# One neighbour fewer for the gather queue in every fifth tile: VectorE columns, moved SyncE rows, and the last rows written apart

## The chip, the cores and the metric

The kernel runs on one core of a Trainium2 chip. The metric is the device time of one execution in microseconds; the median of three runs before the change is 29,957.43 us (29,957.26 to 29,957.63).

## The reference, cut to what matters

A table of 50,001 items is built first. Each item has 32 neighbours; for two embedding tables of width 32 the item attends over its neighbours' rows. The results are then looked up for 16,384 users with 100 history items each.

```python
def _neighbor_attn(E, near_full):
    V = E[near_full]                                   # 32 rows of 32 per item
    scores = jnp.einsum('nd,nkd->nk', E, V) / jnp.sqrt(jnp.float32(GEO_HALF))
    w = jax.nn.softmax(scores, axis=-1)
    return jnp.einsum('nk,nkd->nd', w, V)
...
a_sus = _neighbor_attn(E_in, near_full)
a_inf = _neighbor_attn(E_out, near_full)
hist_bi = jnp.concatenate([a_sus[history], a_inf[history]], axis=-1)
tgt_bi = jnp.concatenate([a_inf[target], a_sus[target]], axis=-1)
h = jnp.concatenate([E_hist[history], hist_bi], axis=-1)
t = jnp.concatenate([E_tgt[target], tgt_bi], axis=-1)
x = h * t[:, None, :]
z = jax.nn.relu(jnp.einsum('bld,hd->blh', x, W1) + b1)
scores = jnp.einsum('blh,h->bl', z, W2[0])
```

Masked exponentials of these scores, their sums and a cosine-like product with the target row give one sigmoid per user.

## The kernel before, in words

There are two stages. The **first** (lines 116 to 430) makes `table` and `ttab` in DRAM, 128 items a tile. 17 tiles (`NSUB`) form an iteration, 23 iterations (`NITER`) the stage: 391 tiles (`NT`). One iteration's neighbour numbers, own rows and history rows are loaded at once by `load`, issued from SyncE in the middle of the iteration before.

A tile's neighbour rows lie in `v`, 128 x 32 x 64 floats, of which there are five buffers. A neighbour row reaches `v` in one of four ways:

- **Gather** (L219): POOL issues an indirect DMA, 128 rows of 256 bytes for one neighbour position k.
- **Column** on ScalarE or VectorE (L239): the embeddings also lie transposed in SBUF as `geoT`, two items to a column of 128. Item numbers are loaded into registers, 32 at a time (`registers`), and each column is copied as 4 bytes per partition into `g`.
- **Column** on TensorE (L234): a matmul of the identity with the column, one for each item, into `pc` in PSUM; `evict` brings it into a `g0` buffer.
- **Row** on SyncE (L214): one DMA of 256 bytes for each of the 128 items, straight into `v`.

Columns become rows in `turn` (TensorE transposes, L262), `even` (ScalarE) and `odd_half` (a predicated copy on VectorE, L279), which picks the right one of a column's two items.

The constants say who does what. `AUX` has a word for each of the last four neighbour positions, four letters for four blocks of 32 items: position 29 wholly by ScalarE, 30 half by ScalarE and half by VectorE, 31 wholly by VectorE. Position 28, "the fourth", goes by `CYCLE = "PSSPS"` and the tile's number modulo 5: TensorE columns in residues 0 and 3, SyncE rows in 1, 2 and 4. So each tile from number 6 on (`NFIRST`) has 28 gathers; the first six have 32, while `geoT` is being filled.

The order on PE, ACT, DVE and SP is written out by hand in the loop over s. Step s issues gathers and columns of tile s, the products, scores and exponents of tile s-1, the weighted sums (`weighted`, L328, `attend`, `attended`) of tile s-2, and `finish` of tile s-3. TensorE's columns of a tile are split between two steps (`by_tensor`). A `v` buffer is free after `weighted` of its tile. At an iteration's end `finish` issues two writes from ScalarE's queue: `table` (L360) and then the last 64 columns of `ttab` (L361).

The **second** stage (L442 on) goes through 128 blocks of 128 users. `target_rows` gathers the target row `t` (L471), `gather` the 100 history rows `h` (L509), again one indirect DMA each. The rest is transposes (L524), products (L526), a matmul (L544), ReLU (L545) and scores (L553). Its gathers read what the first stage wrote.

Of the kernel before, what the change touches and what calls it, by code (L numbers as in the profile page):

```python
# [10 lines left out]
F32 = mybir.dt.float32  # L11
# [7 lines left out]
P = 128  # L19
ITEMS = 50001  # L20
K = 32
G = 32
DE = 64
D = 128
# [7 lines left out]
NSUB = 17  # L32
NITER = -(-ITEMS // (P * NSUB))
# [3 lines left out]

AUX = ("PPPP", "AAAA", "AADD", "DDDD")  # L40
NAUX = len(AUX)
CYCLE = "PSSPS"
NFIRST = 6
ENGINE = {"A": E.Activation, "D": E.DVE, "P": E.PE}
NREG = 32
# [12 lines left out]
def kernel(  # L58
# [13 lines left out]
    nc = tc.nc  # L72
# [43 lines left out]
    with (  # L116
# [15 lines left out]
        def load(it):  # L132
            nidx = n_in.tile([P, NSUB, K], I32, name="nidx")
            nc.sync.dma_start(nidx, near_v[it])
            own = n_in.tile([P, NSUB, 2 * G], F32, name="own")
            nc.sync.dma_start(own, egeo_v[it])

            row = n_in.tile([P, NSUB, D + G], F32, name="row")
            nc.sync.dma_start(row[:, :, 0:DE], ehist_v[it])

            colf = n_p.tile([P, NSUB, NAUX + 1], F32, name="colf")
            coli = n_p.tile([P, NSUB, NAUX], I32, name="coli")
            aux = nidx[:, :, K - NAUX : K]
            nc.vector.tensor_scalar(coli, aux, 1, None, ALU.logical_shift_right)
            nc.vector.tensor_copy(colf[:, :, 1 : NAUX + 1], coli)
            nc.vector.tensor_scalar(
                colf[:, :, 1 : NAUX + 1],
                colf[:, :, 1 : NAUX + 1],  # L150
                4.0,
                float(geoT_at),
                ALU.mult,
                ALU.add,
            )
            nc.vector.tensor_copy(colf[:, :, 0:1], nidx[:, :, K - NAUX : K - NAUX + 1])
            nc.vector.tensor_scalar(
                colf[:, :, 0:1], colf[:, :, 0:1], float(8 * G), None, ALU.mult
            )
            odd = n_in.tile([P, NSUB, NAUX], I32, name="odd")  # L160
            nc.vector.tensor_scalar(odd, aux, 1, None, ALU.bitwise_and)
            n = NSUB * (NAUX + 1)
            col_ps = n_pt.tile([P, 4, P], F32, name="pt")
            nc.tensor.transpose(col_ps[0:n, 0, :], colf.rearrange("p j a -> p (j a)"), ident)
            cols = n_in.tile([n, P], I32, name="cols")
            nc.vector.tensor_copy(cols, col_ps[0:n, 0, :])
            its[it] = (nidx, own, row, odd, cols)
# [28 lines left out]
            )  # L196
            return vals

        def kind(s):
            return "" if s < NFIRST else CYCLE[s % len(CYCLE)]  # L200

        def gather(s):
            it, j = divmod(s, NSUB)
            nidx = its[it][0]
            v = n_v.tile([P, K, 2, G], F32, name="v")
            subs[s].update(v=v)
            if kind(s):
                subs[s]["g"][1:] = [n_g.tile([P, P], F32, name=f"g{a}") for a in range(1, NAUX)]
            k1 = K - NAUX
            if kind(s) == "S":  # L210
                for i0 in range(0, P, NREG):
                    vals = registers(s, 0, E.SP, i0, 0, (ITEMS - 1) * 8 * G)
                    for i in range(NREG):
                        nc.sync.dma_start(  # L214
                            v[i0 + i : i0 + i + 1, k1].rearrange("p t d -> p (t d)").bitcast(U8),
                            egeo_b[:, ds(vals[i], 8 * G)],
                        )
            for k in range(k1 if kind(s) else K):
                nc.gpsimd.indirect_dma_start(  # L219
                    out=v[:, k].rearrange("p t d -> p (t d)"),  # L220
                    out_offset=None,
                    in_=egeo,
                    in_offset=bass.IndirectOffsetOnAxis(ap=nidx[:, j, k : k + 1], axis=0),
                )

        def columns(s, a, i0):

            e = AUX[a][i0 // NREG]
            vals = registers(s, a + 1, ENGINE[e], i0, geoT_at, geoT_at + 4 * (PAIRS - 1))
            g = subs[s]["g"][a]  # L230
            for i in range(i0, i0 + NREG):
                column = geoT_b[:, ds(vals[i - i0] - geoT_at, 4)]
                if e == "P":
                    nc.tensor.matmul(  # L234
                        g[:, i : i + 1], ident, column.bitcast(F32), start=True, stop=True
                    )
                else:
                    copy = nc.scalar.copy if e == "A" else nc.vector.tensor_copy
                    copy(g.bitcast(U8)[:, 4 * i : 4 * i + 4], column)  # L239

        def by_tensor(s, half):
            if s >= NT or kind(s) != "P":
                return
            if half == 0:
                subs[s] = {"g": [None] * NAUX}
                subs[s]["g"][0] = n_pc.tile([P, P], F32, name="pc")
            for i0 in range(half * P // 2, (half + 1) * P // 2, NREG):
                columns(s, 0, i0)

        def evict(s):  # L250
            if kind(s) == "P":
                g = n_g.tile([P, P], F32, name="g0")
                nc.scalar.copy(g, subs[s]["g"][0])  # L253
                subs[s]["g"][0] = g

        def turn(s):
            if not kind(s):
                return
            first = 0 if kind(s) == "P" else 1
            back = n_pt.tile([P, 4, P], F32, name="pt")  # L260
            for a in range(first, NAUX):
                nc.tensor.transpose(back[:, a, :], subs[s]["g"][a], ident)  # L262
            subs[s]["back"] = back[:, first:NAUX, :]
            subs[s]["aux"] = subs[s]["v"][:, K - NAUX + first : K].rearrange("p k t d -> p k (t d)")
            subs[s]["odd"] = its[s // NSUB][3][:, s % NSUB, first:NAUX]

        def even(s):
            it, j = divmod(s, NSUB)
            if kind(s):
                nc.scalar.copy(subs[s]["aux"], subs[s]["back"][:, :, 0 : 2 * G])  # L270
            own_ps = n_ps.tile([P, 1, 2 * G], F32, name="own_ps")
            nc.scalar.copy(own_ps[:, 0, :], its[it][1][:, j, :])  # L272
            subs[s]["own"] = own_ps

        def odd_half(s):
            if not kind(s):
                return
            odd = subs[s]["odd"]
            nc.vector.copy_predicated(  # L279
                subs[s]["aux"],  # L280
                odd.rearrange("p (a o) -> p a o", o=1).to_broadcast([P, odd.shape[1], 2 * G]),
                subs[s]["back"][:, :, 2 * G : 4 * G],
            )

        def products(s):
            v = subs[s]["v"]
            prod = n_p.tile([P, K, 2, G], F32, name="prod")
            nc.vector.tensor_tensor(  # L288
                prod.rearrange("p k t d -> p k (t d)"),
                v.rearrange("p k t d -> p k (t d)"),  # L290
                subs[s]["own"].to_broadcast([P, K, 2 * G]),
                ALU.mult,
            )
            subs[s]["prod"] = prod
# [60 lines left out]
        def finish(s):  # L355
            it, j = divmod(s, NSUB)
            row = its[it][2]
            nc.scalar.copy(row[:, j, D : D + G], row[:, j, DE : DE + G])
            if j == NSUB - 1:
                nc.scalar.dma_start(table_v[it], row[:, :, 0:D])  # L360
                nc.scalar.dma_start(ttab_v[it][:, :, DE:D], row[:, :, DE + G : D + G])  # L361
                del its[it]
            del subs[s]

# [7 lines left out]
        for s in range(NT + 3):  # L372
            if s < NT:
# [1 line left out]
                    load(s // NSUB + 1)  # L375
                subs.setdefault(s, {"g": [None] * NAUX})
                gather(s)
            now = s < NT
            one, two, three = (0 <= s - d < NT for d in (1, 2, 3))

            def act(i):
                if now and kind(s) and i < len(acts):
                    columns(s, *acts[i])
                for q in chunks[:some]:
                    transposed(q)
                del chunks[:some]

            def dve(i):
                if now and kind(s) and i < len(dves):
                    columns(s, *dves[i])  # L390

            act(0)
# [2 lines left out]
            if one:  # L395
                evict(s - 1)
                turn(s - 1)
                even(s - 1)
                odd_half(s - 1)
                products(s - 1)  # L400
            by_tensor(s, 1)
            by_tensor(s + 1, 0)
            dve(0)
# [20 lines left out]
            act(5)  # L424
            if two:
                attended(s - 2)
            for i in range(6, len(acts)):
                act(i)
            if three:
                finish(s - 3)  # L430

# [237 lines left out]
```

## Time and profile before

| what | value |
|---|---|
| median of the timed runs | 29,957.43 us |
| the profiled execution: time, span | 44,478.55 us, 44,476.8 us |
| POOL busy | 22,605.5 us (51%), 23,906 instructions |
| PE busy | 19,148.2 us (43%) |
| DVE busy | 15,032.9 us (34%) |
| ACT busy | 11,097.3 us (25%) |
| granted TensorE clock | 0.843 mean; 1.00 in the first stage, 0.65 in the second |
| first stage, from the first to the last neighbour gather's start | 9.1 to 24,054.2 us |
| second stage, from the first to the last history gather's start | 24,177.1 to 44,438.9 us |
| row transfers from SyncE (L214) | 29,568, of 0.2 KB |
| columns on ACT, on DVE (L239) | 73,920 each |
| TensorE column matmuls (L234), two passes each | 39,424 |

Lines of the groups view give, after the count, the busy time in us and the mean of one in ns, then the idle time of the engine just ahead of them and what ended most of it. Timeline lines give start and length in us, engine, line, operation, what is written and read, how many are merged, and in brackets the idle time before. The time of the profiled execution is a good deal longer than that of the timed runs; counts are the same in both.

### The profile page before, as it was taken

The numbers are of one execution on the slowest core, as the hardware profiler recorded it, in microseconds if no ns is written. First come the engines' busy times: TensorE is split into PE (matmuls) and PEld (weight loads), VectorE is DVE, ScalarE is ACT, GpSimd is POOL, SyncE is SP. The second block draws the span as 40 slices with busy tenths as digits, with TensorE's granted clock in tenths as the row PEclk, the third lists the DMA queues.
The fourth block names the chain that finished last, engine by engine and source line by source line (L and its number), as shares of the span: only waits on it lengthen the run. The fifth ranks groups of instructions, "written<-read, shape, count | busy, mean of one in ns | idle before, by whom it ended". The sixth has DMA issues, their size and how long they took to land. (4 is left out here: it accounts for less than half of the span.)

```text
span 44476.8 us, 458858 instructions
## 1 busy us (share of the span) xinstructions
PE 19148.2 (43%) x85883; PEld 15643.9 (35%) x85883; DVE 15032.9 (34%) x82351; ACT 11097.3 (25%) x80592; POOL 22605.5 (51%) x23906
## 2 busy tenths in 40 slices
PE   2333333333333333333334544555445444554555
PEld 2333333333333333333333333333333333333333
DVE  3444444444444444444444111111111111111112
ACT  2333333333333333333333111111111111111111
POOL 4444444444444444444444655666656656656665
PEclk9999999999999999999999666666666666666666
DMA  1011101111011001111111111111111111111111
GB/s 44 19 19 19 20 19 19 20 19 19 19 19 19 19 19 19 19 19 19 19 19 25 43 42 42 43 43 42 43 42 43 43 42 42 43 42 42 43 43 41
DMA packets 1049451, 1348.20 MB, mean 30 GB/s; under 512 B 595425, under 2 KB 658337, under 8 KB 1046625
## 3 DMA queue, kind: packets, MB, share of 16 engines
q0 software_dynamic: 764800, 1208.31, 12.2%
q1 hardware_dynamic: 130800, 59.23, 0.5%
q10 hardware_dynamic: 151024, 51.31, 0.5%
q14 instruction: 2069, 16.94, 0.1%
q8 instruction: 758, 12.42, 0.1%
HBM read 1278.68 MB, written 51.30 MB: 30 GB/s over the span
## 5 line engine op out<-in xcount | busy, mean ns | idle before, releaser
L219 POOL DMA_INDIRECT v<-in_egeo_dram,nidx x10972 | 10377.5, 946 | 13676.4 <-DVE wv L328 10389.0
L509 POOL DMA_INDIRECT h<-table,hidx x12800 | 12106.3, 946 | 7999.2 <-issue 6458.4
L239 ACT COPY g<-geoT 128x4 uint8 x73920 | 8225.0, 190 | 14294.0 <-issue 12445.4
L239 DVE COPY g<-geoT 128x4 uint8 x73920 | 6838.5, 177 | 10606.6 <-issue 10598.7
L234 PE MATMUL pc<-geoT,ident 128*128 x39424 | 8423.7, 348 | 2160.7 <-issue 2160.0
L234 PEld LDWEIGHTS pc<-geoT,ident 128*128 128x128 f32 x39424 | 8491.6, 332 | 2016.6 <-issue 2014.8
L544 PE MATMUL z_ps<-xT,w1T 128*128 128x512 f32 x6400 | 4908.0, 861 | 5896.2 <-DVE xT L526 4633.2
L526 DVE TENSOR_TENSOR xT<-hT_ps,tT 128x1024 f32<-128x1024 f32 (+1 forms) x1664 | 1969.1, 1183 | 13245.5 <-remote 6985.3
L545 ACT ACTIVATE z<-z_ps,b_sb 128x512 f32<-128x512 f32 x3200 | 2192.9, 687 | 15223.3 <-remote 6927.6
L553 PE MATMUL score<-w_sb,z 128*128 128x1 f32 x25600 | 3873.4, 273 | 4150.4 <-ACT z L545 3432.3
L262 PE MATMUL pt<-ident,g 128*128 128x128 f32 x1309 | 477.1, 442 | 12002.6 <-ACT g L253 5287.3
L553 PEld LDWEIGHTS score<-w_sb,z 128*128 128x128 f32 x25600 | 3878.2, 235 | 4383.7 <-ACT z L545 3628.8
L262 PEld LDWEIGHTS pt<-ident,g 128*128 128x128 f32 x1309 | 251.5, 211 | 12304.8 <-ACT g L253 5362.5
L544 PEld LDWEIGHTS z_ps<-xT,w1T 128*128 128x128 f32 x6400 | 1359.3, 263 | 6314.5 <-DVE xT L526 4897.9
L524 PEld LDWEIGHTS hT_ps<-ident,h 128*128 128x128 f32 x12800 | 2359.8, 200 | 2670.9 <-issue 2489.1
L524 PE MATMUL hT_ps<-ident,h 128*128 128x128 f32 x12800 | 3138.4, 337 | 49.2 <-DVE xT L526 36.2
L529 DVE TENSOR_REDUCE hsum<-h 128x8 f32<-128x1024 f32 (+1 forms) x1664 | 1943.4, 1168 | 0.0
L328 DVE TENSOR_TENSOR wv<-v,ex 128x1024 f32<-128x1024 f32 x782 | 1477.9, 1891 | 0.0
L560 DVE TENSOR_TENSOR ea<-ea,keep 128x100 f32<-128x100 f32 x128 | 33.8, 264 | 3061.3 <-ACT ea L559 2840.7
L288 DVE TENSOR_TENSOR prod<-v,own_ps 128x2048 f32<-128x2048 f32 x391 | 894.5, 2288 | 455.8 <-ACT own_ps L272 152.9
L298 DVE TENSOR_REDUCE sc<-prod 128x64 f32<-128x2048 f32 x391 | 891.8, 2281 | 0.2
L341 DVE TENSOR_REDUCE att<-wv 128x64 f32<-128x2048 f32 x391 | 885.7, 2265 | 8.4 <-issue 8.1
(70 smaller groups left out, 1928.4 us busy)
## 6 DMA issues: line engine op xcount, KB each, us to landing
v<-in_egeo_dram SPq DMA_DIRECT2D x29568, 0.2 KB
h<-table,hidx POOLq DMA_INDIRECT x12800
v<-in_egeo_dram,nidx POOLq DMA_INDIRECT x10972
table<-row ACTq DMA_DIRECT2D x23, 1088.0 KB
own<-in_egeo_dram SPq DMA_DIRECT2D x23, 544.0 KB
row<-in_ehist_dram SPq DMA_DIRECT2D x23, 544.0 KB
ttab<-row ACTq DMA_DIRECT2D x23, 544.0 KB
ttab<-in_etgt_dram ACTq DMA_DIRECT2D x1, 12500.0 KB
```

The costliest lines, as they stand in the source:

```text
L219: nc.gpsimd.indirect_dma_start(out=v[:, k].rearrange("p t d -> p (t d)"), out_offset=None, in_=egeo, in_offset=bass.IndirectOffsetOnAxis(a ...
L234: nc.tensor.matmul(g[:, i : i + 1], ident, column.bitcast(F32), start=True, stop=True)
L239: copy(g.bitcast(U8)[:, 4 * i : 4 * i + 4], column)
L288: nc.vector.tensor_tensor(prod.rearrange("p k t d -> p k (t d)"), v.rearrange("p k t d -> p k (t d)"), subs[s]["own"].to_broadcast([P, K, ...
L328: nc.vector.tensor_tensor(subs[s]["wv"][:, t].rearrange("p d k -> p k d"), subs[s]["v"][:, :, t, :], subs[s]["ex"][0][:, t, :] .rearrange( ...
L509: nc.gpsimd.indirect_dma_start(out=h[:, q, :], out_offset=None, in_=table, in_offset=bass.IndirectOffsetOnAxis(ap=u["hidx"][:, l : l + 1], ...
L524: nc.tensor.transpose(hT_ps[:, q, :], h[:, q, :], ident)
L526: x = nc.vector.tensor_tensor(xT[:, 0:w, :], hT_ps[:, 0:w, :], u["tT"].to_broadcast([D, w, P]), ALU.mult)
L529: s = nc.vector.tensor_reduce(u["hsum"][:, g * LW : g * LW + w], h[:, 0:w, :], AX.X, ALU.add)
L544: nc.tensor.matmul(z_ps, w1T, xT[:, q : q + LG, :], start=True, stop=True)
L545: nc.scalar.activation(z[:, q : q + LG, :], z_ps, AF.Relu, bias=b1_sb)
L553: nc.tensor.matmul(u["score"][:, l : l + 1], z[:, q, :], w2_sb, start=True, stop=True)
```

## The change

The fourth neighbour (position 28) and the fifth from the end (27) now go by two words of their own. `COLUMN = "PD.P."`: position 28 is fetched by TensorE columns in residues 0 and 3, by VectorE columns in residue 1, and by a gather in 2 and 4. `BY_ROW = "S.S.S"`: position 27 is fetched by SyncE rows in residues 0, 2 and 4, and by a gather in 1 and 3. The first entry of `colf`, from which SyncE's addresses come, is taken from position 27 instead of 28. VectorE's new columns stand in four blocks: two after `products`, two after `attended`. In `finish` the `ttab` write now stands ahead of the `table` write, and in the last iteration rows 0 to 15 of each partition are written with tile 15, row 16 with tile 16.

```diff
 AUX = ("PPPP", "AAAA", "AADD", "DDDD")
 NAUX = len(AUX)
-CYCLE = "PSSPS"
+COLUMN = "PD.P."
+BY_ROW = "S.S.S"
...
-            nc.vector.tensor_copy(colf[:, :, 0:1], nidx[:, :, K - NAUX : K - NAUX + 1])
+            nc.vector.tensor_copy(colf[:, :, 0:1], nidx[:, :, K - NAUX - 1 : K - NAUX])
...
-        def kind(s):
-            return "" if s < NFIRST else CYCLE[s % len(CYCLE)]
+        def fourth(s):
+            return COLUMN[s % len(COLUMN)]
+
+        def by_row(s):
+            return s >= NFIRST and BY_ROW[s % len(BY_ROW)] == "S"
...
-            if kind(s):
+            if s >= NFIRST:
                 subs[s]["g"][1:] = [n_g.tile([P, P], F32, name=f"g{a}") for a in range(1, NAUX)]
-            k1 = K - NAUX
-            if kind(s) == "S":
+                if fourth(s) == "D":
+                    subs[s]["g"][0] = n_g.tile([P, P], F32, name="g0")
+            k1 = K - NAUX - 1
+            if by_row(s):
...
-            for k in range(k1 if kind(s) else K):
+            ks = list(range(K))
+            if s >= NFIRST:
+                ks = ks[0 : K - 3]
+                if fourth(s) != ".":
+                    ks.remove(K - 4)
+                if by_row(s):
+                    ks.remove(K - 5)
+            for k in ks:
                 nc.gpsimd.indirect_dma_start(
...
-            e = AUX[a][i0 // NREG]
+            e = AUX[a][i0 // NREG] if a else fourth(s)
...
         def turn(s):
-            if not kind(s):
+            if s < NFIRST:
                 return
-            first = 0 if kind(s) == "P" else 1
+            first = 1 if fourth(s) == "." else 0
...
             nc.scalar.copy(row[:, j, D : D + G], row[:, j, DE : DE + G])
+
+            if j == NSUB - 1 or (it == NITER - 1 and j == NSUB - 2):
+                j0 = NSUB - 1 if it == NITER - 1 and j == NSUB - 1 else 0
+                js = slice(j0, j + 1)
+                nc.scalar.dma_start(ttab_v[it][:, js, DE:D], row[:, js, DE + G : D + G])
+                nc.scalar.dma_start(table_v[it][:, js, :], row[:, js, 0:D])
             if j == NSUB - 1:
-                nc.scalar.dma_start(table_v[it], row[:, :, 0:D])
-                nc.scalar.dma_start(ttab_v[it][:, :, DE:D], row[:, :, DE + G : D + G])
                 del its[it]
...
                 odd_half(s - 1)
                 products(s - 1)
+            if NFIRST <= s < NT and fourth(s) == "D":
+                columns(s, 0, 0)
+                columns(s, 0, NREG)
             by_tensor(s, 1)
             by_tensor(s + 1, 0)
...
             if two:
                 attended(s - 2)
-            for i in range(6, len(acts)):
-                act(i)
+            if NFIRST <= s < NT and fourth(s) == "D":
+                columns(s, 0, 2 * NREG)
+                columns(s, 0, 3 * NREG)
             if three:
                 finish(s - 3)
```

More of the change, by code (lines that the diff above doesn't have):

```diff
@@ L241, in by_tensor @@
         def by_tensor(s, half):
-            if s >= NT or kind(s) != "P":
+            if s < NFIRST or s >= NT or fourth(s) != "P":
                 return
@@ L250, in evict @@
         def evict(s):
-            if kind(s) == "P":
+            if s >= NFIRST and fourth(s) == "P":
                 g = n_g.tile([P, P], F32, name="g0")
@@ L268, in even @@
             it, j = divmod(s, NSUB)
-            if kind(s):
+            if s >= NFIRST:
                 nc.scalar.copy(subs[s]["aux"], subs[s]["back"][:, :, 0 : 2 * G])
@@ L275, in odd_half @@
         def odd_half(s):
-            if not kind(s):
+            if s < NFIRST:
                 return
@@ L377 @@
                 gather(s)
-            now = s < NT
             one, two, three = (0 <= s - d < NT for d in (1, 2, 3))
             def act(i):
-                if now and kind(s) and i < len(acts):
+                if NFIRST <= s < NT and i < len(acts):
                     columns(s, *acts[i])
@@ L388, in dve @@
             def dve(i):
-                if now and kind(s) and i < len(dves):
+                if NFIRST <= s < NT and i < len(dves):
                     columns(s, *dves[i])
```

## The prediction

> **What bounds the kernel now.** I read the page's busy shares and costliest groups first, then the timeline of POOL, then a stretch near the end of the first stage where the other engines run alone.
>
> ```profile
> span 44476.8 us, 458858 instructions
> ...
> L509 POOL DMA_INDIRECT h<-table,hidx x12800 | 12106.3, 946 | 7999.2 <-issue 6458.4
> L219 POOL DMA_INDIRECT v<-in_egeo_dram,nidx x10972 | 10377.5, 946 | 13676.4 <-DVE wv L328 10389.0
> ```
>
> The first surprise is the span: 44,476.8 us (44,478.55 with what lies around it), while the median of the timed runs is 29,957.4. The profiled execution is half as long again, so its waits cannot be read as those of a timed run. The reader should take the counts from here: 10,972 neighbour gathers, 12,800 history gathers and 128 target gathers (L471) make 23,900 on one queue.
>
> ```profile
> 24020.47 0.94 POOL L219 DMA_INDIRECT v<-in_egeo_dram,nidx  x1 [23.20 <-DVE wv L328]
> 24021.72 0.95 POOL L219 DMA_INDIRECT v<-in_egeo_dram,nidx  x1 [0.30 <-issue]
> ...
> 24054.24 0.95 POOL L219 DMA_INDIRECT v<-in_egeo_dram,nidx  x1 [0.30 <-issue]
> ```
>
> These are the last tile's 28 gathers. Once POOL has its buffer nothing disturbs it: 24020.47 to 24054.24 is 33.77 us for 27 intervals, **1.2507 us per gather** (0.95 busy, 0.30 issue). History gathers have the same pitch where none waits (24177.13, 24178.38, 24179.65). Times 23,899 intervals this is 29,890 us. That leaves 67 us of the median; POOL's first gather starts at 9.1, and the last one starts 38 us before the span's end. So about 18 us, or 28 if the true pitch is 0.4 ns shorter, is left for everything else. A timed run is POOL issuing gathers back to back in both stages. Where then do the profile's waits come from?
>
> ```profile
> 10040.70 0.17 DVE L239 COPY g<-geoT 128x4 uint8 x1 [1.23 <-issue]
> 10041.42 0.19 ACT L239 COPY g<-geoT 128x4 uint8 x1 [1.24 <-issue]
> ...
> 24060.01 43.24 SPq L214 DMA_DIRECT2D v<-in_egeo_dram  x112
> ...
> 24062.81 3.22 ACT L239 COPY g<-geoT 128x4 uint8 x32 [1.44 <-issue]
> 24064.40 2.37 DVE L239 COPY g<-geoT 128x4 uint8 x32
> ```
>
> In the middle of the stage ACT and DVE each finish one column per 1.4 us, in lock step; in the clean stretch 32 take 3.14 to 3.22 and 2.37 us. I take the lock step for a cost of recording, which a timed run does not pay (if it did, 29,957 would be impossible), and price columns from the clean stretch.
>
> ```profile
> 24060.00:24118.00 58.00, 54.18 (x254) 53.70 (x254) 51.62 (x428) 41.51 (x409) 0.00 (x0) 1.00 0.01 2
> 24061.16 0.21 ACT L272 COPY own_ps<-own 128x64 f32<-128x64 f32 x1
> 24089.60 0.22 ACT L272 COPY own_ps<-own 128x64 f32<-128x64 f32 x1
> 24119.07 0.22 ACT L272 COPY own_ps<-own 128x64 f32<-128x64 f32 x1
> 24147.69 0.22 ACT L272 COPY own_ps<-own 128x64 f32<-128x64 f32 x1
> ```
>
> The copy into own_ps comes once a step, so free-running steps last 28.4, 29.5 and 28.6 us. POOL needs 28 x 1.2507 = 35.0 for a tile. The stretch of two steps (columns PE, PEld, DVE, ACT, POOL) shows PE 27.1 and DVE 25.8 busy a step. The others have about 6 us to spare in each tile.
>
> [...]the 0.95 us never varies, whatever the transfer does, so POOL's pitch is a cost of issuing and only fewer gathers lower it. [...]the gathers at 24020.47 and 24021.72 keep their pitch beside 32 columns that DVE copies from 24020.06 in 2.62 us, and the history stage, which has no columns, has the same pitch[...]. [...]the row gives 177 ns for one 4-byte column, but 32 follow each other in 2.37 us (74 ns), and this pitch is what I use.
>
> **The change, part by part.** From tile 6 on there are 385 tiles, 77 of each residue mod 5.
>
> *Gathers.* Before, every such tile has 28: columns k 0 to 27, the fourth neighbour (k = 28) going to TensorE or SyncE. After, the list starts from 29; k = 28 leaves where the fourth is a column (residues 0, 1, 3), k = 27 where SyncE fetches it (0, 2, 4). So residue 0 has 27 and all others 28. The saving is one gather in five tiles: 77 x 1.2507 = **96.3 us** (the built program has 23,823 instead of 23,900). All lies on the queue that sets the end.
>
> *SyncE.* Row transfers stay at three tiles in five, from residues 1, 2, 4 to 0, 2, 4, each 128 transfers. The pattern has one adjacent pair as before. From the clean line 43.24/112 = 0.39 us each, with register loads: 49 us a tile, 148 in five, against POOL's 175 before and 139 x 1.2507 = 173.8 after. Covered; if the cover goes, products at L288 are late next. Zero.
>
> *TensorE.* Its column tiles stay residues 0 and 3; 77 more transposes of 0.44 us, beside POOL. Zero; uncovered, 34 us.
>
> *DVE, the added load.* Residue 1 gets 4 blocks of 32 columns. At 2.37 us each that is 9.5 us; if no register load is hidden, the price is ACT's pitch of consecutive blocks (10002.22, 10006.29, 10010.36: 4.1 us), 16.4. I take 12. That step becomes about 29 + 12 = 41 us, over POOL's 35. What queues behind: two blocks stand ahead of scores (L298) and of the wv products of tile s-2, two ahead of the next step's predicated copy; so wv, which frees a v buffer, is some 6 us late. There are five v buffers: tile s is freed midway in step s+2, some 20 us after POOL begins tile s+2, and POOL wants it at s+5. That is 105 - 20 = 85 us of slack. Five steps take 4 x 29 + 41 = 157 us against 173.8, so the lag is gone one step later. I cost it at nothing; without that cover it is 77 x 12 = 924 us.
>
> *Table writes.* In 22 iterations two writes merely swap order. In the last, rows 0 to 15 of each partition are written a step earlier and row 16 alone.
>
> ```profile
> 24159.55 0.22 ACT L358 COPY row<-row 128x32 f32<-128x32 f32 x1 [5.12 <-DVE row L348]
> ...
> 24165.64 0.53 ACTq L360 DMA_DIRECT2D table<-row  x1
> 24166.26 2.08 ACTq L361 DMA_DIRECT2D ttab<-row  x1
> ...
> 24174.53 0.94 POOL L471 DMA_INDIRECT t<-ttab,tidx  x1 [119.34 <-DMA ttab<-row]
> ```
>
> POOL starts 8.9 us after the writes are issued. The 16 rows can go at 24159.8, landing near 24168.7; row 16 goes near 24166.5 and a small load (hidx, issued 24173.90, used 24176.80) takes 2.9, so 24169.4. Saving 5 us; the ends are 0 (the pieces wait for each other) and 8.
>
> Sum: 96.3 + 5 = 101 us off. Against the median, which the pitch explains to within 20 us: 29,957.4 - 101 = **29,856 us**. The profiled span may move otherwise[...].
>
> **Rivals.** *Slower: DVE's slack is what pays for the iteration ends.*
>
> ```profile
> ACT g L239 <- DMA ttab<-row: 1831.0, 22, 95.7
> ```
>
> At each iteration's end ACT sits 83 us before its table write, while SyncE is still issuing row transfers. If a timed run has this wait too, the old steps win it back (17 x (35.0 - 29.0) = 102 us an iteration), but the new average step of 31.4 us wins back only 17 x (34.8 - 31.4) = 58. Then 25 us an iteration are lost once the 85 us of buffers are used up, in about 19 iterations: 475 - 101, so 30,330 us. It decides where the wait exceeds 58 us. Against it: SyncE in a timed run needs 148 of 174 us and should be well ahead by then; in the profile it is held up by recording.
>
> *No change: the steps, not POOL, set the first stage* at 35 us; then the 77 gathers are hidden and 29,952 remains. Against it: steps of 28.4 to 29.5, and no other reason why two stages should sum to POOL's pitch.
>
> *It does less than it says.* The words speak of three tiles in five twice, yet the count gives one gather in five tiles; this is already in the sum.
>
> **How the numbers follow.** The forecast has 0.82, its own range 29,845 to 29,872 (transition 8 to 0, some lost microseconds). Slower by the iteration ends[...], 0.09; no change, 0.06; lags that eat part of the gain, 0.03. A measurement tells 0.2%, 60 us, from no change; the forecast is 0.34%. Faster 0.83, same 0.08, slower 0.09. Range 29,835 to 29,915: the forecast's, and partial losses.
>
> **What would show it.** L219 with x10895 and L509 unchanged, both at 1.25 us where nothing waits; DVE column copies up by 9,856; PE transposes up by 77; the first target gather some 6 instead of 8.9 us after the last write is issued. Wrong: a timed median above 29,900 with those counts, which would mean POOL waits for v buffers in timed runs.

## The result, and the profile after

The changed kernel takes 29,856.5 us (29,855.4 to 29,857.8), the kernel before beside it 29,957.6 us (29,956.5 to 29,958.4): **101.1 us less**, ratio 0.9966 with an interval of 0.9955 to 0.9978. The prediction said 29,856.

The page of the changed kernel, its span, busy shares and the two lines of gathers. The lines of the kernel have moved: neighbour gathers are now L234, history gathers L531, target gathers L493, columns L254, products L303, `wv` L343:

```profile
span 29855.8 us, 468978 instructions
## 1 busy us (share of the span) xinstructions
PE 21844.2 (73%) x85960; PEld 16222.4 (54%) x85960; DVE 14647.7 (49%) x92207; ACT 10175.8 (34%) x80592; POOL 22540.9 (75%) x23829
...
L531 POOL DMA_INDIRECT h<-table,hidx x12800 | 12107.9, 946 | 3902.9 <-issue 3490.4
L234 POOL DMA_INDIRECT v<-in_egeo_dram,nidx x10895 | 10311.3, 946 | 3332.4 <-issue 3208.7
```

This profiled execution is not stretched: 29,855.8 us of span, 29,857.5 with what lies around it. So it shows directly what had to be inferred from the stretched one. POOL is busy for 75% of the span, and of the idle time before its history and neighbour gathers 89 and 96% is "issue". POOL's list of waits (us in total, number of waits, the longest one) has no line for wv, which stood first with 10,389 us before:

```profile
POOL h L531 <- issue: 3490.4, 11447, 0.4
POOL v L234 <- issue: 3208.7, 10513, 0.3
...
POOL t L493 <- DMA table<-row: 22.6, 1, 22.6
```

No single wait before a gather in this list is longer than 0.4 us, save 22.6 us at the hand-over between the stages and 7.4 us for the first load. The first neighbour gather starts at 8.7 and the last at 13,644.1 us: 13,635.4 us for 10,894 intervals, 1.2516 us each. The counts are those that the prediction listed: 10,895 and 12,800 gathers, 9,856 more VectorE columns (83,776), 77 more TensorE transposes (1,386). Columns copied beside gathers run at nearly their clean speed, 32 in 2.42 us here beside the prediction's 2.37, and the gathers keep their pitch, 1.25 us from 6006.36 to 6007.61:

```profile
6006.31 2.42 DVE L254 COPY g<-geoT 128x4 uint8 x32
6006.36 0.94 POOL L234 DMA_INDIRECT v<-in_egeo_dram,nidx  x1 [0.30 <-issue]
6007.61 0.95 POOL L234 DMA_INDIRECT v<-in_egeo_dram,nidx  x1 [0.30 <-issue]
...
6011.60 2.58 ACT L254 COPY g<-geoT 128x4 uint8 x26 [1.64 <-issue]
```

The kernel before takes 29,898 to 29,958 us on some chips and 44,193 to 44,520 us on others, in timed runs too, so each experiment is read only against the kernel before on its own chip. I call the first chips quick and the second slow.

### The profile page after: what moved, and what is told of

It reads as the page before. It is cut to its first block, busy times and chain, and to the rows that moved or that the text cites. A ratio compares the mean times of both kernels' runs of the same rounds, so it can differ in the third digit from the quotient of the medians.

```text
span 29855.8 us, 468978 instructions
## 1 busy us (share of the span) xinstructions
PE 21844.2 (73%) x85960; PEld 16222.4 (54%) x85960; DVE 14647.7 (49%) x92207; ACT 10175.8 (34%) x80592; POOL 22540.9 (75%) x23829
## 4 chain that ended last, share of the span: by engine, by line
POOL 30%; issue 16%; DMA 10%; PE 8%; SPq 4%; DVE 3%; ACT 0%; DVEq 0%; POOLq 0%; ACTq 0%
POOL h L531 23%; DMA h<-table,hidx 9%; POOL v L234 7%; PE z_ps L566 4%; SPq L222 3%; PE score L575 2%; PE hT_ps L546 2%; DVE xT L548 1%; DVE g L254 1%; SPq L193 1%; DMA v<-in_egeo_dram,nidx 1%; DVE hsum L551 0%; DVE prod L303 0%; DVE sc L313 0%; DVEq L193 0%
## 5 line engine op out<-in xcount | busy, mean ns | idle before, releaser
L531 POOL DMA_INDIRECT h<-table,hidx x12800 | 12107.9, 946 | 3902.9 <-issue 3490.4
L234 POOL DMA_INDIRECT v<-in_egeo_dram,nidx x10895 | 10311.3, 946 | 3332.4 <-issue 3208.7
L254 ACT COPY g<-geoT 128x4 uint8 x73920 | 7265.2, 189 | 3172.9 <-issue 2704.2
L546 PE MATMUL hT_ps<-ident,h 128*128 128x128 f32 x12800 | 5076.2, 415 | 3190.9 <-DMA h<-table,hidx 3011.1
L254 DVE COPY g<-geoT 128x4 uint8 x83776 | 6539.1, 196 | 1095.9 <-issue 1091.1
L546 PEld LDWEIGHTS hT_ps<-ident,h 128*128 128x128 f32 x12800 | 2454.4, 195 | 8481.3 <-DMA h<-table,hidx 7830.7
L566 PE MATMUL z_ps<-xT,w1T 128*128 128x512 f32 x6400 | 5785.7, 1005 | 22.1 <-DVE xT L548 21.8
L575 PEld LDWEIGHTS score<-w_sb,z 128*128 128x128 f32 x25600 | 4411.3, 259 | 0.5 <-issue 0.5
L575 PE MATMUL score<-w_sb,z 128*128 128x1 f32 x25600 | 4097.6, 282 | 0.0
L566 PEld LDWEIGHTS z_ps<-xT,w1T 128*128 128x128 f32 x6400 | 1883.2, 354 | 109.8 <-issue 70.4
L303 DVE TENSOR_TENSOR prod<-v,own_ps 128x2048 f32<-128x2048 f32 x391 | 894.5, 2288 | 1337.8 <-DMA v<-in_egeo_dram 668.2
L343 DVE TENSOR_TENSOR wv<-v,ex 128x1024 f32<-128x1024 f32 x782 | 1474.2, 1886 | 0.0
L285 ACT COPY v<-pt 128x256 f32<-128x256 f32 (+1 forms) x385 | 135.1, 351 | 1625.4 <-PE pt L277 1609.0
```

The source lines that it names most:

```text
L234: nc.gpsimd.indirect_dma_start(out=v[:, k].rearrange("p t d -> p (t d)"), out_offset=None, in_=egeo, in_offset=bass.IndirectOffsetOnAxis(a ...
L343: nc.vector.tensor_tensor(subs[s]["wv"][:, t].rearrange("p d k -> p k d"), subs[s]["v"][:, :, t, :], subs[s]["ex"][0][:, t, :] .rearrange( ...
L531: nc.gpsimd.indirect_dma_start(out=h[:, q, :], out_offset=None, in_=table, in_offset=bass.IndirectOffsetOnAxis(ap=u["hidx"][:, l : l + 1], ...
L546: nc.tensor.transpose(hT_ps[:, q, :], h[:, q, :], ident)
L566: nc.tensor.matmul(z_ps, w1T, xT[:, q : q + LG, :], start=True, stop=True)
L575: nc.tensor.matmul(u["score"][:, l : l + 1], z[:, q, :], w2_sb, start=True, stop=True)
```

## The experiments

### On quick chips: is it the number of gathers?

The changed kernel again, with no edit, on another chip, as the base for what follows.

> The changed kernel itself, beside the kernel before on the chip of the experiments. Theory (two conditions, and what bounds the kernel differs between them): where the kernel before takes 29,957 us, 29,856.5; where it takes 44,200 to 44,280 us, the VectorE step is paid in full and the gathers are hidden, as in the kernel with the gathers' change alone (1.0091), and the split writes take off a little: 1.007 to 1.010 of the kernel before. Rival (the change gains about 100 us under any condition): 0.998.

Measured: 29,796.9 us beside 29,898.2, ratio 0.9966 (0.9953 to 0.9979), 101.4 us less. The chip is 0.2% faster as a whole and the gain is the same.

Then the changed kernel without VectorE's columns; residue 1 gathers its fourth neighbour again.

```diff
-COLUMN = "PD.P."
+COLUMN = "P..P."
```

> COLUMN = "P..P." again (no VectorE columns for the fourth neighbour; residue 1 gathers 29; 23,900 gathers as before), meant for the condition of 29,898 to 29,957 us. Theory: only the split writes' 4.5 us remain, 0.9998 of the kernel before, 96 us over the changed kernel, and the step of residue 1 falls from 43 to about 30 us. Rival A (the gain is the moved rows' or the writes'): 0.9966. Rival B (27 and 29 gathers in turn make somebody wait): above 1.0005.

Measured: 29,896.3 us beside 29,901.4, ratio 0.9998 (0.9989 to 1.0008); 11 runs between 29,893.4 and 29,897.0 against 29 runs between 29,899.8 and 29,903.8. The 5.1 us are what remains when the gathers are back at 23,900: the gain of the split writes and the moved rows together. The other 96.3 of the 101.4 us go with the 77 gathers, 1.251 us each. The two gains come from two chips, on which the kernel before differs by 3 us, so the agreement with the prediction to a tenth is chance. Rival A (0.9966) falls; rival B (above 1.0005) falls by the runs, which all lie below those of the kernel before, though the interval reaches 1.0008.

### On quick chips: how far does DVE's cover reach?

Two kernels with the same 23,746 gathers, 154 fewer than before. One gives residue 2 to VectorE like residue 1:

```diff
-COLUMN = "PD.P."
+COLUMN = "PDDP."
```

> COLUMN = "PDDP." again (VectorE columns in residues 1 and 2; 23,746 gathers as in the mixed kernel), meant for the condition of 29,898 to 29,957 us. If gathers alone counted: 0.9934, as the mixed kernel. Theory (DVE's cover is finite: 2 x 43 + 3 x 28.8 = 172.4 us in five steps against POOL's 172.5, and 21 us more at each iteration's end that nothing wins back): POOL waits for v buffers, 0.998 to 1.006.

The other splits both residues' columns between VectorE and ScalarE:

```diff
-COLUMN = "PD.P."
+COLUMN = "PMMP."
+MIX = "DADA"
...
-            e = AUX[a][i0 // NREG] if a else fourth(s)
+            e = AUX[a][i0 // NREG] if a else "P" if fourth(s) == "P" else MIX[i0 // NREG]
```

(the two tests `fourth(s) == "D"` around its blocks, and the one in `gather`, become `"M"`).

> COLUMN = "PMMP." again (residues 1 and 2 by two VectorE and two ScalarE blocks each; 23,746 gathers), meant for the condition in which the kernel before takes 29,898 to 29,957 us. Theory (gathers count while the steps stay under POOL's pitch; five steps 2 x 36.4 + 3 x 28.8 = 159 us against 138 x 1.25 = 172.5): two gathers in five tiles saved, 0.9934 of the kernel before, 96 us under the changed kernel. Rival (ScalarE, whose blocks take 4.1 us, becomes late): no better than the changed kernel's 0.9966.

Measured on one chip: two VectorE tiles 29,951.5 us, ratio 1.0017 (1.0010 to 1.0024), **slower** than before; mixed 29,705.9 us, ratio 0.9935 (0.9915 to 0.9954), the fastest of all kernels here, 195.5 us under the kernel before. On this same chip the mixed kernel takes 190.5 us less than the one without VectorE's columns, for 154 gathers fewer: 1.24 us a gather. Between the two kernels of this section the gathers are the same, and the times are 245.6 us apart. POOL's waits with two VectorE tiles show where they are:

```profile
POOL v L234 <- DVE wv L343: 185.7, 61, 16.3
...
POOL t L493 <- DMA table<-row: 91.1, 1, 91.1
```

With mixed tiles there is no wait for wv and the hand-over is back at 22:

```profile
POOL t L494 <- DMA table<-row: 22.1, 1, 22.1
```

185.7 + 69.0 at the hand-over is 255, close to the 246 between the two. (A wait stands in the place of a gap of 0.3 us that POOL has anyway; 61 of these are 18 us.) The products, once a step, give the steps of the kernel with two VectorE tiles:

```profile
9037.29 2.29 DVE L303 TENSOR_TENSOR prod<-v,own_ps 128x2048 f32<-128x2048 f32 x1 [0.42 <-DMA v<-in_egeo_dram]
9079.54 2.29 DVE L303 TENSOR_TENSOR prod<-v,own_ps 128x2048 f32<-128x2048 f32 x1
9125.55 2.29 DVE L303 TENSOR_TENSOR prod<-v,own_ps 128x2048 f32<-128x2048 f32 x1
9153.92 2.29 DVE L303 TENSOR_TENSOR prod<-v,own_ps 128x2048 f32<-128x2048 f32 x1
```

42.3, 46.0 and 28.4 us. Over the whole stage the means by residue 0 to 4 are 29.6, 43.0, 43.0, 29.5 and 30.3, together 175.4 us, against POOL's 138 x 1.249 = 172.4. The missing 3.0 us times 77 is 231 us. The plain steps are as long as the theory had them: the medians by residue are 28.7, 42.7, 42.7, 28.2 and 29.8, together 172.1. What the means have more comes from the steps that hold the writes at an iteration's end, one in seventeen: they are 10 us longer than the median of their residue, 220 us over the stage. So both halves of the theory hold: the plain steps use up POOL's time, and nothing is left for the iterations' ends. What decides in these kernels is the sum over five tiles and the waits that come more seldom, not whether one step is longer than POOL's tile: the changed kernel has one of 43.0 us beside POOL's 35.0 and waits for no buffer.

### On quick chips: is it the buffers that carry the long step?

```diff
-        tc.tile_pool(name="n_v", bufs=5) as n_v,
+        tc.tile_pool(name="n_v", bufs=3) as n_v,
```

> The changed kernel with three v buffers again, meant for the condition of 29,898 to 29,957 us. Theory (each buffer is worth 35 us of lag; 80 us in the middle with five becomes 10, and below zero behind the VectorE step and an iteration's end): POOL waits for wv, 29,900 to 30,700 us, 1.000 to 1.025 of the kernel before. Rival (the buffers are not what hides the VectorE step): 0.9966.

Measured: 31,408.2 us, ratio 1.0498 (1.0477 to 1.0518). POOL now waits for wv, and so do the products, on SyncE's rows and on gathers:

```profile
POOL v L234 <- DVE wv L343: 1542.1, 152, 26.2
...
DVE prod L303 <- DMA v<-in_egeo_dram,nidx: 1390.9, 118, 29.0
DVE prod L303 <- DMA v<-in_egeo_dram: 1352.0, 104, 27.7
```

In the changed kernel:

```profile
DVE prod L303 <- DMA v<-in_egeo_dram: 668.2, 156, 9.3
DVE prod L303 <- DMA v<-in_egeo_dram,nidx: 622.0, 118, 29.2
```

The buffers are needed, but the loss against the kernel before, 5.0%, is twice the upper end that I had given (2.5%). The number had let POOL alone run short of buffers. SyncE does too: its own queue waits 2,972 us for wv instead of 1,365, so its rows start late and the products wait for them, twice as long as with five. This edit takes lag from two queues at once and does not measure the VectorE step alone; the kernel before was not run with three buffers, so how much of the loss it would have had too stays open.

### On slow chips: the other bound

Seven edits ran where the kernel before takes 44,193 to 44,520 us. The stretched profile shown ahead of the prediction, 44,476.8 us, is of this kind. The gathers' change alone, that is the changed kernel with the old `finish`:

```diff
-            if j == NSUB - 1 or (it == NITER - 1 and j == NSUB - 2):
-                j0 = NSUB - 1 if it == NITER - 1 and j == NSUB - 1 else 0
-                js = slice(j0, j + 1)
-                nc.scalar.dma_start(ttab_v[it][:, js, DE:D], row[:, js, DE + G : D + G])
-                nc.scalar.dma_start(table_v[it][:, js, :], row[:, js, 0:D])
             if j == NSUB - 1:
+                nc.scalar.dma_start(table_v[it], row[:, :, 0:D])
+                nc.scalar.dma_start(ttab_v[it][:, :, DE:D], row[:, :, DE + G : D + G])
                 del its[it]
```

> The changed kernel with finish as it was before: table then ttab, and the last iteration's 17 rows written at its end. Theory: only the hand-over between the stages grows, from 23.5 us between the last neighbour gather and the first target gather to about 28, so 29,861 us. Rival (the pieces wait for each other, so splitting gains nothing): 29,856.5. Rival (the order of the two writes matters in every iteration): more than 10 us away.

Measured: 44,670.0 us beside 44,276.7, ratio **1.0091** (1.0074 to 1.0108). The numbers expected of this run and of the three that follow were for a quick chip and are not tested here; the sign is the point. POOL's waits:

```profile
POOL v L234 <- DVE wv L343: 10575.6, 379, 69.6
```

POOL waits for a buffer 379 times in 391 tiles, so the steps set the time. The 77 saved gathers do not show, and the time is 393 us longer. The steps of residue 1 last 71.9 us, the other four 58.0 to 60.8. The changed kernel without VectorE columns (`P..P.`, as above):

> The changed kernel with COLUMN = "P..P.": VectorE's new columns are gone and residue 1 gathers its fourth neighbour again (29 gathers), so POOL issues 23,900 as before, while the moved SyncE rows and the split last writes stay. Theory (POOL issues back to back at 1.2512 us; moving rows costs nothing): 29,856.5 + 77 x 1.2512 = 29,953 us, and the step of residue 1 falls from 43 to about 30 us. Rival A (the gain came from the moved rows or the writes, not from the number of gathers): it stays near 29,857. Rival B (uneven tiles of 27 and 29 gathers make somebody wait): above 29,965.

Measured: 44,257.7 us, ratio 1.0003 (0.9994 to 1.0011). Its step of residue 1 is 60.0 us. The difference of the two kernels is 412 us, or 5.4 us for each of 77 tiles (they differ in `finish` too). That is less than half of the 11.9 us by which the VectorE step is longer: the other four steps are 1.0 to 2.8 us shorter than without it, so part of it is won back.

The kernel before with the new `finish` alone (the edit just shown, the other way round, in the kernel before), and the changed kernel with two VectorE tiles (`PDDP.`):

> The kernel before with the new finish alone (ttab first, rows 0 to 15 a step earlier in the last iteration). Theory: 29,957.5 - 4.5 = 29,953 us, POOL's 23,900 gathers unchanged. Rival (no gain from splitting): 29,957.5. In its profile, unless recording slows it, POOL's gathers should follow each other at 1.25 us with no wait for a v buffer.

> The changed kernel with COLUMN = "PDDP.": residue 2 too gets its fourth neighbour by VectorE columns, so 77 gathers fewer (23,746) and two steps of 43 us in five. If gathers alone counted: 29,856.5 - 96.3 = 29,760 us. Theory (the cover of DVE's extra work is finite): five steps take 2 x 43 + 3 x 28.8 = 172.4 us against POOL's 138 x 1.2512 = 172.7, nothing is left to win back the wait at each iteration's end (21 us in the changed kernel), so POOL begins to wait for v buffers: 29,900 to 30,150 us, slower than the 29,760 of gathers alone and likely slower than 29,856.

Measured: writes alone 0.9995 (0.9986 to 1.0004), which on this chip cannot be told from nothing; two VectorE tiles 1.0241 (1.0224 to 1.0258). With none, one and two VectorE tiles the ratios are 1.0003, 1.0091 and 1.0241.

The mixed tiles and the three buffers also ran on a slow chip:

> The changed kernel with COLUMN = "PMMP.": in residues 1 and 2 the fourth neighbour comes by columns of which VectorE copies two blocks and ScalarE two, so 23,746 gathers, 77 fewer than the changed kernel. Two conditions are known by now. Where the kernel before takes 29,957 us (POOL back to back): theory says gathers count as long as the steps stay under POOL's pitch; a mixed step is about 29 + 2 x 3.8 = 36.4 us on DVE, five steps 2 x 36.4 + 3 x 28.8 = 159 against 172.7, so 29,856.5 - 96.3 = 29,760 us. Rival (the third column source makes ACT late, whose blocks take 4.1 us each, and POOL waits): above 29,857. Where the kernel before takes 44,277 us (every engine held to one small instruction in 0.7 to 1.4 us, POOL waiting for a v buffer in every tile): the saved gathers are hidden and the 2 x 77 x 128 columns cost, as with two VectorE tiles: 44,700 to 45,300 us.

> The changed kernel with three v buffers in place of five. In the changed kernel's profile a buffer was free 63 us at the least, 80 us in the middle, before POOL wanted it. Theory: each buffer is worth one tile of POOL, 35 us, so with three the middle is 10 us and the worst below zero; SyncE's rows, which run ahead only as far as buffers are free, come late too. Where the kernel before takes 29,957 us: 29,950 to 30,700 us, with POOL waiting for wv in the tiles behind the VectorE step and behind an iteration's end. Rival (the five buffers are not what hides the VectorE step): 29,857. Where the kernel before takes 44,277 us, POOL already waits for a buffer in every tile, and with five buffers the products come 195 us after their gather; three buffers still cover a gather of 35 us, so no more than 0.5% over the 44,670 of the same gathers with five.

Measured: mixed 44,563.7 us beside 44,193.0, ratio 1.0083 (1.0067 to 1.0100), cheaper than I expected (44,700 at the least) though it adds as many columns as two VectorE tiles; shared between two engines they cost 371 us over the kernel before instead of 1,061, each on its own chip. Three buffers 1.0633 (1.0615 to 1.0651), where I expected at most 1.014 (0.5% over 44,670). What they held was again the lead of SyncE's rows: the products now wait 2,631 us for these, and 30 us in the kernel with the gathers' change alone and five buffers.

```profile
DVE prod L303 <- DMA v<-in_egeo_dram: 2630.6, 207, 27.5
```

At last, from the mixed kernel, three mixed tiles in five:

```diff
-COLUMN = "PMMP."
+COLUMN = "PMMPM"
```

> The mixed kernel with COLUMN = "PMMPM": residue 4 mixed too, 23,669 gathers. In the kernel with two VectorE steps, where the steps set the time, they lasted 29.6, 43.0, 43.0, 29.5 and 30.3 us by residue. A mixed step has two blocks of about 3.75 us more on DVE than a plain one: 37.1 us. Theory: five steps 3 x 37.1 + 29.6 + 29.5 = 170.4 us against POOL's 137 x 1.249 = 171.1, so POOL still sets the pace, if barely: 96 us under the two mixed tiles, 0.990 of the kernel before, up to 0.993 if a mixed step is 1.5 us longer. Rival (ScalarE or TensorE ends a mixed step late once there is no plain step behind it): POOL waits for wv by 150 us or more, no better than two mixed tiles, 0.9935 or above. In the condition in which the kernel before takes some 44,200 us: 1.012 to 1.02.

This too met a slow chip: 45,255.8 us beside 44,519.9, ratio 1.0167 (1.0150 to 1.0184), inside what was expected there. Whether it would beat two mixed tiles on a quick chip stays open.

## Why the prediction was right, point by point

**The bound.** 23,899 intervals of POOL's pitch explain the median; read from 28 gathers in a stretched execution, the pitch was 1.2507 us, and 10,894 intervals of an unstretched one give 1.2516. The kernel without VectorE's columns and the changed one differ by the price of the gathers, as far as the runs can tell. The rest of the changed kernel's span is 8.7 us ahead of the first gather, 23.5 at the hand-over and 18.6 from the last gather's start; for this last stretch the prediction had taken 38 us from the stretched execution. The free-running steps of 28.4 to 29.5 us are confirmed where the steps set the time: 28.2 to 29.8 for the plain steps of the kernel with two VectorE tiles.

**Gathers.** 96.3 us predicted; 96.3 measured, as the 101.4 us of the whole change less the 5.1 us that remain without the VectorE columns, each on its own chip. VectorE's added columns did not slow the gathers: the pitch is 1.2516 us in the first stage, with the columns, and 1.2508 in the second, which has none. The 0.95 us of a gather is 0.947 in the median in both stages, 943 to 1,100 ns with 64 floats a row in the first and 943 to 1,039 with 128 in the second. That the pitch is a cost of issuing, which only fewer gathers lower, was my reading of this: the runs show what fewer gathers save, 1.24 to 1.25 us each, and no run shows another way.

**SyncE and TensorE at zero.** 5.1 us of gain remain with the rows moved to residues 0, 2, 4, about what the sum gave the writes, so it seems that moving them cost nothing. No quick run has the moved rows or the writes alone, so two terms that cancel are not ruled out. For TensorE's 77 transposes no run stands alone either.

**DVE's added load.** I took 12 us for four blocks, between 9.5 and 16.4. In the changed kernel's timeline of a step with them, blocks that follow each other:

```profile
6023.60 2.48 DVE L254 COPY g<-geoT 128x4 uint8 x32 [1.28 <-issue]
6027.35 2.49 DVE L254 COPY g<-geoT 128x4 uint8 x32 [1.26 <-issue]
6031.15 2.46 DVE L254 COPY g<-geoT 128x4 uint8 x32 [1.31 <-issue]
```

The pitch is 3.75 to 3.80 us: between two blocks that follow each other VectorE is idle for 1.3 us. I take this for the part of the register load that isn't hidden; no run shows it apart. The step lasts 43.0 us on average instead of 41. The term was 2 us small, and covered. The products of tile s come on average 11.6 us after its last gather has been issued in residue 1, 5.7 in residue 2 and 3.6 to 4.7 elsewhere; "gone one step later" was nearly so. Counting from the end of the second wv of tile s to the first gather of tile s+5, the buffer is free 80 us ahead in the middle, 63 at the least. The prediction had 85.

**The slower rival.** It was the right mechanism to fear. ScalarE's wait at the iteration's end exists in the unstretched execution:

```profile
ACT g L254 <- DMA table<-row: 465.5, 22, 30.4
```

21 us each, under the 58 us from which it would decide. The step that holds it is 12 us longer than the median of its residue, and most of the next six are shorter than theirs, on average by 3.2, 2.5, 1.7, 0.5, 0.0 and 2.7 us: the slack pays for it, as the rival says. One VectorE tile leaves room for it; with two, plain steps of 172.1 us beside POOL's 172.4 left none, and the kernel was slower than before.

**The stretched profile.** Here a reason was wrong and its use right. I took the lock step of ACT and DVE for a cost of recording, which timed runs do not pay. But the changed kernel was recorded instruction by instruction, 468,978 of them, in 29,857.5 us, and on slow chips timed runs take as long as the stretched profile. So it isn't recording as such. What was sound was the arithmetic: no stretched execution fits into 29,957 us. Had the timed runs come from a slow chip, the "no change" rival's bound (the steps set the first stage) would have been the right one, and the sign slower: 1.0091 for the gathers' change alone. That the result was measured at the quick pace was luck: the prediction had no term for the other one. The sentence that SyncE is "held up by recording" in the profile falls with the same reason.

**Table writes.** 5 us predicted, 5.1 with the rows moved as well. By themselves the writes ran on a slow chip alone, where their gain is lost in the noise, and no profile has the kernel before at the quick pace. So the size fits the sum and is not shown apart. The hand-over, from the timeline:

```profile
13658.70 0.39 ACTq L378 DMA_DIRECT2D ttab<-row  x1
13659.14 1.15 ACTq L379 DMA_DIRECT2D table<-row  x1
...
13665.18 0.46 ACTq L379 DMA_DIRECT2D table<-row  x1
...
13667.61 0.95 POOL L493 DMA_INDIRECT t<-ttab,tidx  x1 [22.57 <-DMA table<-row]
```

The first target gather comes 2.4 us after the last write is issued; the sum had used 2.9. (The closing list said "some 6", which did not agree with the sum.)

## What to carry to other kernels

Take the busiest queue's undisturbed pitch times its count and hold it against the timed median, before believing the waits of an execution that is much longer than the timed runs. Add up the steps over the pattern's period, with the waits that come more seldom, and hold the sum against the bound's. Here one step of 43.0 us in five cost nothing, the 77 gathers bringing 1.251 us each; with two, 175.4 us stood beside POOL's 172.4 and the kernel was 50 us slower than before; the same columns shared between two engines brought 1.24 us a gather again. Say on which chip a verdict was won: with another bound the gathers' part of the edit lost 0.9%.

## What the runs showed of the hardware that was not expected

The same program has two paces: of the five chips that the experiments met, two ran it in 29,898 to 29,901 us and three in 44,193 to 44,520, each in all its runs. Each chip was met on one occasion only, so whether the pace belongs to the chip or to the occasion is not shown. In the slow pace TensorE, VectorE and ScalarE finish few instructions while POOL's gathers run, and many while POOL waits: VectorE's columns are back at full speed 4.8 us after a tile's last gather has been issued (the median of 382 such waits in the first stage). TensorE has 3 matmuls in the first of the stretches below, with 17 gathers in it, and 48 in the 10 us from 10,010, where POOL waits until 10,017.9. Two stretches of the kernel before, its stretched execution, columns PE, PEld, DVE, ACT, POOL, each busy time with its count, then the granted clock, the share of the DMA engines and GB/s:

```profile
10030.00:10050.00 20.00, 0.49 (x3) 0.57 (x2) 2.99 (x15) 2.77 (x15) 15.12 (x17) 1.00 0.16 27
10065.00:10080.00 15.00, 0.47 (x1) 0.18 (x1) 14.66 (x108) 10.73 (x107) 0.00 (x0) 1.00 0.01 2
```

A stretch of the changed kernel at the quick pace, with gathers going on:

```profile
6035.00:6055.00 20.00, 20.00 (x95) 20.00 (x96) 19.66 (x141) 14.73 (x147) 15.14 (x16) 1.00 0.16 29
```

With 16 or 17 gathers in 20 us, DVE ends 15 instructions in one and 141 in the other, ACT 15 and 147, PE 3 and 95, while the gathers' own pitch, the granted clock (1.00) and the share of the DMA engines (0.16) are the same. What on the slow chips makes the engines wait is not shown by any run here; recording by itself is ruled out, as is the granted clock in this stage, and a bound of the DMA engines is unlikely.
